# Tasks on fixed places in a software-pipelined attention kernel on one Trainium2 core

## The chip, the cores and the metric

The kernel runs on one core of one Trainium2 chip. A core has a matrix engine (TensorE, in the profile PE, with PEld for its weight loads) and three engines that work on rows of numbers: VectorE (DVE), ScalarE (ACT) and GpSimd (POOL). SyncE (SP) issues transfers. Each engine works through its own list of instructions in the order in which the program holds them, and the engines wait for each other through semaphores. Matrix products land in PSUM banks; VectorE and ScalarE carry the results from there into the on-chip memory.

The metric is the device time in microseconds, the median of several runs. A profile is taken from one execution; its "span" runs from the first to the last recorded instruction.

## The reference, cut to what matters

The input is a batch of 8 images of 32 x 32 x 256 in 32-bit floats; an image is taken as N = 1024 tokens of C = 256 channels. Layer 0 is attention with four heads, each 256 wide, layer 1 a single attention with 32-wide keys:

```python
# layer 0
qkv = einsum('bnc,cd->bnd', xf, W_qkv).reshape(B, N, 4, 3 * C)
q, k, v = split(qkv, 3, axis=-1)
atten = softmax(einsum('bihd,bjhd->bijh', q, k) * C ** -0.5, axis=2)
res = einsum('bijh,bjhd->bihd', atten, v).reshape(B, N, 4 * C)
x = einsum('bnd,dc->bnc', res, W_out) + b_out + xf
# layer 1
f, g, h = x @ Wf + bf, x @ Wg + bg, x @ Wh + bh      # 32, 32 and 256 wide
y = gamma * (softmax(g @ f.T, axis=-1) @ h) + x
```

## The kernel before, in words

**Folding.** At the start the weights of each head are multiplied together (`fold_weights`, L281): Wq with Wk, so that the scores are x (WqWk) x^T, and Wv with Wout, so that values need no projection of their own and a head's result is projected once. Four such foldings are done: head 0's ahead of the loop, the other three inside its first step.

**Seven products.** `seven` (L222) is the core of layer 0. It multiplies two matrices, each cut into 2 x 2 blocks, with seven block products in place of eight. The price is sums of blocks: four of the left matrix (`sum_a`, L192: s1, s2, s3, s4), four of the right one (`sum_b`, L202), and additions on the way out of PSUM. The seven products are made in three tasks, over three PSUM banks x, y and z:

- task one: products 1, 6 and 5 into x, y, z. Then ScalarE copies x out as e (L258), and VectorE makes u = y + e (L252). u and e are kept.
- task two: products 2 and 7, added by the matrix unit onto what stands in x and y. The first of them can only go when e has been copied. Then x goes out on ScalarE as block 11 (L264), and VectorE makes v = y + e and block 22 = z + v.
- task three: products 4 and 3, added onto y and z, which may only start once v and block 22 have read them. Then VectorE makes blocks 21 and 12.

Every sum that is made of an earlier result must therefore be ready when TensorE comes to its product: product 6 takes s2, product 5 s1, product 7 s3, product 3 s4. Where two tasks of one `seven` stand close together in TensorE's list, it waits for an evacuation; the more other tasks stand between them, the more time that evacuation has.

Three things go through `seven`: a head's queries (`queries`, L442; banks named psx_q and so on, and the four block sums `qs` as a separate list of pieces), the scores (`scores`, L472; banks psx, psy, psz), and the product of probabilities and values (`products`, L556; banks psx_y, psy_y, psz_y).

**Steps.** The work is a list of steps (L773). A unit is one head of one image (`Layer0`) or one image's layer 1 (`Layer1`), and a unit has two steps, one for each block of 512 queries. The list runs over images: heads 0 to 3 of image b, then layer 1 of image b-1. The last layer 1 follows after the loop. A step is a pipeline stage. While step i makes its own scores, it also does, for the units of steps i-1 and i-2:

- scores of step i: for each of two groups of keys three tasks of `seven`, so six (called S0a, S0b, S0c, S1a, S1b, S1c below), with exponentials on ScalarE (L489, L490, L264);
- sums of step i-1's probabilities (`sums`, L507): the four block sums as pieces of VectorE (L528), and two pieces called keys, which make the row sums of the softmax: `first` adds the s tiles (L533), `second` adds further (L538, L539), lets GpSimd add over partitions (L541), and turns the row into columns with two transfers on SP (L545, L548);
- products of step i-1 (three tasks);
- for step i-2, `invert` (L552), one reciprocal of the columns, and `project` (L577): two tasks that multiply with the folded value weights into a bank called po, each followed by two VectorE instructions (L596) that scale and add into the image's rows.

Where they fall due, a step also carries: the next head's queries and their sums; the residual in four pieces (`residual`, L378; head 0's second block); the block sums of the image as values (`value_sums`, L362); the transposes of an image (`transpose_rows`, L331, each four transposes and one ScalarE copy) and its block sums as keys (`key_sums`, L346). A layer-1 step has two score tasks of four products each with ScalarE copies (L659) and a maximum over keys (L693 to L701, with a reduction on GpSimd that shares the buffer tags `rs` and `rb` with the row sums of layer 0), five softmax pieces (subtractions on VectorE, exponentials on ScalarE), and, one step later, four products tasks of eight matmuls (`row_products`, L719); its first block also carries the values in four tasks (`values`, L628, banks named pr_v).

**What sets the order.** The order of TensorE, VectorE and ScalarE is that of the Python text: the pools are opened with a manual schedule for these three engines (L762). PSUM banks come from two pools, six for `seven` and the layer-1 scores and products, two (tag psm) for projections, transposes and values; within a pool a tile takes the next free bank. In a step, the order comes from `weave` (L746), which takes lists of tasks, each with a stretch (lo, hi) of the step. It spreads the tasks of each list evenly over the list's stretch and sorts all by that position:

```python
at = [
    (lo + (hi - lo) * (i + 0.5) / len(l), k, t)
    for k, (l, lo, hi) in enumerate(lists) for i, t in enumerate(l)
]
```

The loop over the steps (L791 to L844) fills the lists. Scores go over (0, 1), products of the step before over (0.4, 1.0), its sums over (0.08, 0.32) and (0.4, 0.7), keys over (0.7, 0.95), projections over (0.4, 0.8), queries over (0.07, 0.39). In a layer-0 step after a layer-0 step this gives S0a, S0b, S0c, S1a with the projections and products among S1a, S1b and S1c. All three products tasks of a block, and with them the two readings of its last banks, are in the one step.

Of the kernel before, what the change touches and what calls it, by code (L numbers as in the profile page):

```python
# [20 lines left out]
def kernel(  # L21
# [52 lines left out]
    B, H, W, C = x.shape  # L74
# [38 lines left out]
    rows, rows1 = {}, {}  # L113

    def load_x(b, parts=1):
        t = tile_of("rows", [P, NT, C], f"x_{b}")
        n = HT // parts
        for k in range(NBLK):
            for i in range(parts):
                nc.sync.dma_start(  # L120
                    t[:, k * HT + i * n : k * HT + (i + 1) * n, :].rearrange("p t c -> p (t c)"),
                    x_v[b][:, k, ts(i, n * C)],
                )
        rows[b] = t
# [87 lines left out]
    def a_operands(blocks, sums):  # L212
        a11, a12, a21, a22 = blocks
        s1, s2, s3, s4 = sums
        return dict(zip((1, 2, 3, 4, 5, 6, 7), (a11, a12, s4, a22, s1, s2, s3)))
# [113 lines left out]
    xT_of, x1T_of, xblocks, vblocks = {}, {}, {}, {}  # L329
# [32 lines left out]
    def value_sums(b):  # L362

        made = {}

        def piece(i):
            if i == 0:
                r = rows[b]
                t = tile_of("xt", [P, 4, NT // 2, P], f"xt_{b}")
                blocks = [r[:, ts(j, NT // 2), ts(c, P)] for j in range(2) for c in range(CC)]  # L370
                sums = [t[:, k] for k in range(4)]
                made["l"] = sum_b(sums, *blocks)
                vblocks[b] = b_operands(blocks, sums)
            made["l"][i]()

        return [partial(piece, i) for i in range(4)]

    def residual(b):  # L378


        def piece(i):
            if i == 0:
                rows1[b] = tile_of("rows", [P, NT, C], f"x1_{b}")
            nc.vector.tensor_tensor(
                rows1[b][:, ts(i, 2), :], rows[b][:, ts(i, 2), :],
                bout_sb.unsqueeze(1).broadcast_to([P, 2, C]), ALU.add,
            )

        return [partial(piece, i) for i in range(NT // 2)]
# [46 lines left out]
    class Layer0:  # L436
        def __init__(self, b, h):
            self.b, self.h, self.name = b, h, f"{b}_{h}"
            self.p, self.y, self.r = {}, {}, {}
            self.first = (b * HEADS + h) * NBLK * HT  # L440

        def queries(self):  # L442
# [64 lines left out]
        def sums(self, blk):  # L507


            n = f"{self.name}_{blk}"  # L510
            tt = nc.vector.tensor_tensor
            made = {}

            def start():
                half = NT // 2
                p = self.p[blk]
                blocks = [p[:, ts(j, half), ts(e, HB)] for e in range(2) for j in range(2)]
                t = tile_of("ss", [P, 2, half, HB], f"ss_{n}")
                s2 = tile_of("s2", [P, half, HB], f"s2_{n}")
                s3 = tile_of("s3", [P, half, HB], f"s3_{n}")  # L520
                sums = [t[:, 1], s2, s3, t[:, 0]]
                self.pblocks = a_operands(blocks, sums)
                made["t"], made["l"] = t, sum_a(sums, *blocks)

            def piece(i):
                if i == 0:
                    start()
                made["l"][i]()  # L528

            def first():  # L530
                t = made["t"]
                made["m"] = m = tile_of("m0", [P, 2, 2, HB], f"m_{n}")
                tt(m, t[:, :, 0:2, :], t[:, :, 2:4, :], ALU.add)  # L533

            def second():
                m = made["m"]
                r = tile_of("rs", [P, 2, HB], f"rs_{n}")
                tt(r, m[:, :, 0, :], m[:, :, 1, :], ALU.add)  # L538
                tt(r[:, 0, :], r[:, 0, :], r[:, 1, :], ALU.add)  # L539
                t = tile_of("rb", [P, NB], f"rb_{n}")  # L540
                nc.gpsimd.partition_all_reduce(  # L541
                    t, r.rearrange("p e i -> p (e i)"), P, bass_isa.ReduceOp.add
                )
                line = tile_of("line", [1, NB], f"line_{n}")
                nc.sync.dma_start(line, t[0:1, :])  # L545
                self.r[blk] = st = tile_of("st", [P, HT], f"st_{n}")
                with nc.allow_non_contiguous_dma(reason="a row of sums turns into columns"):
                    nc.sync.dma_start(st, line.rearrange("o (t p) -> p (o t)", p=P))  # L548

            return [partial(piece, i) for i in range(4)], [first, second]  # L550
# [5 lines left out]
        def products(self, blk):  # L556


            def out(c, e):
                if blk not in self.y:  # L560
                    self.y[blk] = tile_of("y", [P, CC, NB], f"y_{self.name}_{blk}")
                return self.y[blk][:, c, ts(e, HB)].unsqueeze(1)

            return seven(
                f"y_{self.name}_{blk}", HB, 1,
                lambda number: [
                    (0, vblocks[self.b][number][:, j, :], self.pblocks[number][:, j, :])
                    for j in range(NT // 2)
                ],
                {  # L570
                    "11": partial(out, 0, 0), "12": partial(out, 1, 0),
                    "21": partial(out, 0, 1), "22": partial(out, 1, 1),
                },
                NARROW, nc.scalar.copy,
            )
# [170 lines left out]
    def weave(*lists):  # L746
# [6 lines that stand above are left out]
        for _, _, t in sorted(at, key=lambda x: x[:2]):  # L753
            t()
# [22 lines left out]
    final = Layer1(B - 1)  # L777
# [7 lines left out]
    def is_l0(s):  # L785
        return s is not None and isinstance(s[0], Layer0)

    def step(k):
        return steps[k] if 0 <= k < len(steps) else None

    for i, (a, blk) in enumerate(steps):  # L791
        l0 = isinstance(a, Layer0)
        one, two, nxt = step(i - 1), step(i - 2), step(i + 1)
        lists = []
        if l0:
            lists.append((a.scores(blk), 0, 1))
            if a.h == 2 and blk == 0 and a.b + 1 < B:
                load_x(a.b + 1)
            if a.h == 0 and blk == 1:
                lists.append((residual(a.b), 0.3, 1))  # L800
                if a.b > 0:
                    lists.append((value_sums(a.b), 0, 0.3))
        else:
            tasks, pieces = a.scores(blk)
            lists.append((tasks, 0.02, 0.3))
            lists.append((pieces, 0.4, 1))
        if is_l0(one):
            u, k = one
            sums, keys = u.sums(k)
            lists.append((sums[:2], 0.08, 0.32))  # L810
            lists.append((sums[2:], 0.4, 0.7))
            lists.append((keys, 0.7, 0.95))
            lists.append((u.products(k), 0.4, 1.0))
        elif one is not None:
            lists.append((one[0].products(one[1]), 0.3, 1))
        if is_l0(two):
            u, k = two
            lists.append(([partial(u.invert, k)], 0.34, 0.36))
            lists.append((u.project(k), 0.4, 0.8))
        if i == 0:  # L820
            lists.append((fold_weights(1) + fold_weights(2) + fold_weights(3), 0, 1))

        if is_l0(nxt) and blk == NBLK - 1:
            queries, qsums = nxt[0].queries()
            lists.append((queries, 0.07, 0.39))
            lists.append((qsums, 0.45, 0.95))

        change = l0 and a.h == HEADS - 1
        if (change and a.b == 0 or not l0) and blk == 0 and a.b + (1 if l0 else 2) < B:
            b = a.b + (1 if l0 else 2)  # L830
            lists.append((transpose_rows(b, rows, xT_of, 0), 0.02, 0.35))
            lists.append((key_sums(b), 0.5, 0.8))

        if change and a.b > 0:
            if blk == 0:
                lists.append((transpose_rows(a.b - 1, rows1, x1T_of, 1), 0.02, 0.4))
            else:
                lists.append((nxt[0].queries(), 0.05, 0.4))
        if not l0 and blk == 0:
            lists.append((a.values(), 0.1, 0.9))  # L840
        if nxt is None:
            lists.append((transpose_rows(B - 1, rows1, x1T_of, 1), 0.82, 0.9))
            lists.append((final.queries(), 0.9, 1))
        weave(*lists)  # L844


    count = const.tile([P, 1], F32, tag="count", name="count")
# [79 lines left out]
    with tc.If(bad > 0), ExitStack() as general:  # L927
# [5 lines left out]
        for b in range(B):  # L933
# [9 lines left out]
            a = Layer1(b)  # L943
# [37 lines left out]
```

## Time and profile before

| what | value |
|---|---|
| median of 3 runs | 2511.67 us (2510.96 to 2516.9) |
| the profiled execution's own time | 2508.59 us |
| its span | 2506.8 us |
| its mean granted TensorE clock | 0.990 |
| busy: PE | 2411.3 us |
| busy: DVE | 1580.1 us |
| busy: ACT | 617.6 us |
| busy: POOL | 250.7 us |
| transfers, busiest queue | 3.1% of what 16 transfer engines could do in the span |

The page has several views. The first gives each engine's busy time, its share of the span and its number of instructions. Another follows the chain of work back from the last instruction and says how much of the span each engine held. The groups of instructions show, for a line of the kernel and an engine, what is written from what, the number of times, the busy time, the mean of one, and the idle time of that engine ahead of them with what ended most of it. A name such as psy stands for the bank y of scores, psy_y of products, psy_q of queries, po for projections, pr_v for values, pa_l for layer 1's products. The view of waits lists an engine's idle time by the instruction that ended it: total, number, longest. The view by stretch gives, for a part of the span, its length and then for PE, PEld, DVE, ACT and POOL the busy time with the number of instructions, then the granted clock, the busy share of the transfer engines and the GB/s they moved. In the timeline a line begins with its start and its duration in us; what stands in brackets is the idle time before it and what ended that.

### The profile page before, as it was taken

The page shows a single profiled execution, that of the slowest core. Times are in us where ns is not written, and L with a number is a line of the kernel's source. Part 1 is how long each engine was busy: PE and PEld are TensorE (multiplying, and loading weights), DVE is VectorE, ACT ScalarE, POOL GpSimd, SP SyncE. Part 2 cuts the span into 40 slices and gives each one's busy share as a digit, 9 for nine tenths or more (in the row PEclk, how much of TensorE's full clock was granted, in tenths as well). Part 3 has the DMA queues.
Part 4 walks back from the last instruction along what each step waited for, and adds up shares of the span by engine and source line. Part 5 has one row for each costly group of instructions (what it writes and reads, how often), then busy time and mean ns, then how long its engine had stood idle before and what let it go on. Part 6 is the DMA issues. An engine that isn't in the chain of part 4 may idle for free.

```text
span 2506.8 us, 26004 instructions
## 1 busy us (share of the span) xinstructions
PE 2411.3 (96%) x10608; PEld 1965.0 (78%) x10608; DVE 1580.1 (63%) x2477; ACT 617.6 (25%) x1001; POOL 250.7 (10%) x93
## 2 busy tenths in 40 slices
PE   8999999999999999999999999999899999999998
PEld 6788878877788777887778868788687886878876
DVE  5666666665666656666566665666666666566664
ACT  2222212232222322223222232222322223222232
POOL 0111101110111101111011110111101111011110
PEclk9999999999999999999999999999999999999999
DMA  3000000000000000000000000000000000000000
GB/s 112 1 1 1 1 17 1 1 1 29 6 1 1 1 34 1 1 1 1 34 1 1 1 1 34 1 1 1 1 34 1 1 1 1 17 1 1 1 6 30
DMA packets 43536, 23.64 MB, mean 9 GB/s; under 512 B 36048, under 2 KB 38096, under 8 KB 43408
## 3 DMA queue, kind: packets, MB, share of 16 engines
q1 hardware_dynamic: 43408, 21.90, 3.1%
q8 instruction: 85, 1.39, 0.2%
q14 instruction: 43, 0.35, 0.0%
HBM read 13.37 MB, written 8.52 MB: 9 GB/s over the span
## 4 chain that ended last, share of the span: by engine, by line
PE 80%; DVE 14%; ACT 5%; issue 1%; DMA 0%; SPq 0%; DVEq 0%; ACTq 0%
PE psy L235 12%; PE psy_y L235 11%; PE pa_l L726 9%; PE psx L235 8%; PE po L585 8%; PE psx_y L235 8%; PE psz L235 7%; PE psz_y L235 6%; PE psy_q L235 3%; PE psz_q L235 2%; PE psx_q L235 2%; DVE m L533 2%; DVE p L252 2%; ACT s_l L659 1%; DVE v L252 1%; ACT p L489 1%
## 5 line engine op out<-in xcount | busy, mean ns | idle before, releaser
L541 POOL PARTITION_ALL_REDUCE rb<-rs x64 | 214.5, 3352 | 1825.5 <-DVE rs L539 1825.5
L235 PE MATMUL psx<-q,x0T 128*128 128x256 f32 x1024 | 270.6, 387 | 24.7 <-ACT e L258 24.1
L489 ACT ACTIVATE p<-p 128x1024 f32<-128x1024 f32 x128 | 135.5, 1058 | 633.1 <-DVE p L252 633.1
L235 PE MATMUL psy<-qs,xs 128*128 128x256 f32 x1024 | 269.2, 386 | 1.7 <-DVE qs L460 1.7
L235 PE MATMUL psy_y<-s,xt 128*128 128x256 f32 x1024 | 247.4, 385 | 19.2 <-DVE s L528 19.2
L235 PE MATMUL psz<-q,xs 128*128 128x256 f32 x1024 | 262.8, 379 | 0.0
L235 PEld LDWEIGHTS psx<-q,x0T 128*128 128x128 f32 x1024 | 194.0, 192 | 72.1 <-ACT e L258 33.2
L585 PE MATMUL po<-wvo,y 128*128 128x256 f32 x1024 | 241.9, 379 | 0.0
L235 PE MATMUL psx_y<-p,x 128*128 128x256 f32 x1024 | 241.9, 379 | 0.0
L596 DVE SCALAR_TENSOR_TENSOR x<-po,inverse,x 128x256 f32<-128x256 f32 x256 | 112.0, 479 | 205.3 <-PE po L585 205.3
L235 PEld LDWEIGHTS psy_y<-s,xt 128*128 128x128 f32 x1024 | 196.8, 193 | 49.0 <-DVE s L528 18.5
L726 PE MATMUL pa_l<-v_l,s_l 128*128 128x257 f32 x1024 | 230.4, 380 | 1.8 <-DVE v_l L634 1.8
L235 PEld LDWEIGHTS psy<-qs,xs 128*128 128x128 f32 x1024 | 199.1, 195 | 30.6 <-DVE qs L460 2.1
L726 PEld LDWEIGHTS pa_l<-v_l,s_l 128*128 128x128 f32 x1024 | 194.2, 190 | 34.0 <-issue 5.2
L585 PEld LDWEIGHTS po<-wvo,y 128*128 128x128 f32 x1024 | 194.6, 190 | 26.5
L235 PEld LDWEIGHTS psx_y<-p,x 128*128 128x128 f32 x1024 | 194.6, 190 | 26.5
L235 PEld LDWEIGHTS psz<-q,xs 128*128 128x128 f32 x1024 | 194.6, 190 | 26.4
L252 DVE TENSOR_TENSOR u<-psy,e 128x512 f32<-128x512 f32 x128 | 88.5, 692 | 138.0 <-ACT e L258 78.0
L264 ACT ACTIVATE p<-psx 128x512 f32<-128x512 f32 x128 | 76.4, 597 | 321.7 <-PE psx L235 321.5
L258 ACT COPY e<-psx 128x512 f32<-128x512 f32 x128 | 74.0, 578 | 305.4 <-PE psx L235 305.4
L235 PE MATMUL psy<-qs,x0T 128*128 128x256 f32 x512 | 134.0, 384 | 13.7 <-DVE v L252 13.7
L252 DVE TENSOR_TENSOR v<-psy,e 128x512 f32<-128x512 f32 x128 | 88.5, 692 | 86.9 <-PE psy L235 86.7
(108 smaller groups left out, 3183.9 us busy)
## 6 DMA issues: line engine op xcount, KB each, us to landing
out_dram<-x SPq DMA_DIRECT2D x15, 512.0 KB, 2.6
x<-in_x_dram SPq DMA_DIRECT2D x14, 512.0 KB, 4.6
w<-in_L_conv_W_qkv_dram SPq DMA_DIRECT2D x4, 768.0 KB
x<-in_x_dram SPq DMA_DIRECT2D x4, 256.0 KB, 4.8
w<-in_L_conv_W_out_dram SPq DMA_DIRECT2D x4, 256.0 KB, 9.7
line<-rb SPq DMA_DIRECT2D x64, 2.0 KB
st<-line SPq DMA_DIRECT2D x64, 2.0 KB, 2.1
out_dram<-x SPq DMA_DIRECT2D x4, 128.0 KB, 2.3
```

The source lines that it names most:

```text
L235: nc.tensor.matmul(banks[k][:, ts(i, w)], lhsT=lhsT, rhs=rhs, start=first and n == 0, stop=True, skip_group_check=True,)
L252: nc.vector.tensor_tensor(dst, shaped(banks[k]), shaped(other), ALU.add)
L258: nc.scalar.copy(scratch("e"), banks["x"])
L264: copy(outs["11"](), shaped(banks["x"]))
L489: exp(both, both)
L533: tt(m, t[:, :, 0:2, :], t[:, :, 2:4, :], ALU.add)
L541: nc.gpsimd.partition_all_reduce(t, r.rearrange("p e i -> p (e i)"), P, bass_isa.ReduceOp.add)
L585: nc.tensor.matmul(pm[:, ts(j, C)], lhsT=self.y[blk][:, c, ts(2 * t2 + j, P)], rhs=folded[self.h][1][:, c, :], start=(c == 0), stop=(c == ...
L596: nc.vector.scalar_tensor_tensor(acc, pm[:, ts(j, C)], inverse[:, n : n + 1], acc, ALU.mult, ALU.add)
L659: nc.scalar.copy(soft.tile()[:, j0 + r, :], pm)
L726: nc.tensor.matmul(pm[:, : C + 1], lhsT=p[:, j, ts(ti, P)], rhs=v[:, j, : C + 1], start=(j == 0), stop=(j == NT - 1),)
```

## The change

The loop no longer builds lists with stretches for `weave` (which stays for what follows the loop). Each task is given a place, a number, by `put(tasks, *at)`, and the step runs its tasks sorted by place, those of equal place in the order in which they were put. In a layer-0 step the six score tasks stand at 0, 2, 4, 6, 8 and 10, the first two products tasks of the step before at 5 and 9, the projections of the step before that at 3 and 7.

Two other things change with it. The third products task of a block is no longer in the step of the other two; it comes one step later, at place 1 (0 in a layer-1 step). So `Layer0` keeps the tasks in `products_of` by block, and `pblocks`, the operands of the products, is kept by block too. And the pieces of VectorE (sums, keys, query sums, residual, value sums, key sums, `invert`, softmax pieces) each have a place of their own; s4 now goes with s1 and s2, ahead of s3, which stands at 8.2.

The whole change:

```diff
--- before.py
+++ after.py
@@ -437,6 +437,7 @@
         def __init__(self, b, h):
             self.b, self.h, self.name = b, h, f"{b}_{h}"
             self.p, self.y, self.r = {}, {}, {}
+            self.products_of, self.pblocks = {}, {}
             self.first = (b * HEADS + h) * NBLK * HT
 
         def queries(self):
@@ -519,7 +520,7 @@
                 s2 = tile_of("s2", [P, half, HB], f"s2_{n}")
                 s3 = tile_of("s3", [P, half, HB], f"s3_{n}")
                 sums = [t[:, 1], s2, s3, t[:, 0]]
-                self.pblocks = a_operands(blocks, sums)
+                self.pblocks[blk] = a_operands(blocks, sums)
                 made["t"], made["l"] = t, sum_a(sums, *blocks)
 
             def piece(i):
@@ -564,7 +565,7 @@
             return seven(
                 f"y_{self.name}_{blk}", HB, 1,
                 lambda number: [
-                    (0, vblocks[self.b][number][:, j, :], self.pblocks[number][:, j, :])
+                    (0, vblocks[self.b][number][:, j, :], self.pblocks[blk][number][:, j, :])
                     for j in range(NT // 2)
                 ],
                 {
@@ -788,60 +789,74 @@
     def step(k):
         return steps[k] if 0 <= k < len(steps) else None
 
+
+
+
     for i, (a, blk) in enumerate(steps):
         l0 = isinstance(a, Layer0)
         one, two, nxt = step(i - 1), step(i - 2), step(i + 1)
-        lists = []
+        places = []
+
+        def put(tasks, *at):
+            assert len(tasks) == len(at)
+            places.extend(zip(at, range(len(places), len(places) + len(at)), tasks))
+
         if l0:
-            lists.append((a.scores(blk), 0, 1))
-            if a.h == 2 and blk == 0 and a.b + 1 < B:
-                load_x(a.b + 1)
-            if a.h == 0 and blk == 1:
-                lists.append((residual(a.b), 0.3, 1))
-                if a.b > 0:
-                    lists.append((value_sums(a.b), 0, 0.3))
+            put(a.scores(blk), 0, 2, 4, 6, 8, 10)
         else:
             tasks, pieces = a.scores(blk)
-            lists.append((tasks, 0.02, 0.3))
-            lists.append((pieces, 0.4, 1))
+            put(tasks, *((0.5, 2.5) if blk == 0 else (0.5, 1.5)))
+            put(pieces, *((6.6, 7.6, 8.6, 9, 9.5) if blk == 0 else (5.2, 6.2, 7.8, 8.8, 9)))
+        if is_l0(two):
+            u, k = two
+            put(u.products_of[k][2:], 1 if l0 else 0)
+            put([partial(u.invert, k)], 1.1 if l0 else 0.3)
+            put(u.project(k), *((3, 7) if l0 else (2, 6) if blk == 0 else (3, 7)))
         if is_l0(one):
             u, k = one
             sums, keys = u.sums(k)
-            lists.append((sums[:2], 0.08, 0.32))
-            lists.append((sums[2:], 0.4, 0.7))
-            lists.append((keys, 0.7, 0.95))
-            lists.append((u.products(k), 0.4, 1.0))
+            u.products_of[k] = u.products(k)
+            put(sums[:2] + sums[3:], *((2.2, 3.2, 4.2) if l0 else (1.2, 2.2, 3.2)))
+            put(sums[2:3], 8.2 if l0 else 7)
+            put(keys, *((6.2, 7.2) if l0 else (5.2, 6.2)))
+            put(u.products_of[k][:2], 5, 9 if l0 else 8)
         elif one is not None:
-            lists.append((one[0].products(one[1]), 0.3, 1))
-        if is_l0(two):
-            u, k = two
-            lists.append(([partial(u.invert, k)], 0.34, 0.36))
-            lists.append((u.project(k), 0.4, 0.8))
+            put(one[0].products(one[1]), *((3, 5, 7, 9) if l0 else (1, 4, 6, 8)))
         if i == 0:
-            lists.append((fold_weights(1) + fold_weights(2) + fold_weights(3), 0, 1))
+            fold = fold_weights(1) + fold_weights(2) + fold_weights(3)
+            put(fold, *[0.3 + 0.6 * n for n in range(len(fold))])
 
         if is_l0(nxt) and blk == NBLK - 1:
             queries, qsums = nxt[0].queries()
-            lists.append((queries, 0.07, 0.39))
-            lists.append((qsums, 0.45, 0.95))
-
+            put(queries, *((1.5, 3.5, 4.5) if l0 else (2.5, 4.5, 6.5)))
+            put(qsums, *((5.2, 6.5, 7.5, 8.5) if l0 else (7.2, 7.5, 8.2, 8.5)))
+
+        if l0 and a.h == 0 and blk == 1:
+            put(residual(a.b), 5.3, 6.3, 7.3, 8.6)
+            if a.b > 0:
+                put(value_sums(a.b), 0.2, 0.4, 1.2, 1.4)
+        if l0 and a.h == 2 and blk == 0 and a.b + 1 < B:
+            load_x(a.b + 1)
         change = l0 and a.h == HEADS - 1
-        if (change and a.b == 0 or not l0) and blk == 0 and a.b + (1 if l0 else 2) < B:
-            b = a.b + (1 if l0 else 2)
-            lists.append((transpose_rows(b, rows, xT_of, 0), 0.02, 0.35))
-            lists.append((key_sums(b), 0.5, 0.8))
+        if change and a.b == 0 and blk == 0:
+            put(transpose_rows(1, rows, xT_of, 0), 2.5, 4.5, 6.5, 8.5)
+            put(key_sums(1), 8.7, 9.2, 9.5, 9.8)
+        if not l0 and blk == 0 and a.b + 2 < B:
+            put(transpose_rows(a.b + 2, rows, xT_of, 0), 1, 1.5, 3, 3.5)
+            put(key_sums(a.b + 2), 7.2, 8.2, 9.2, 9.4)
 
         if change and a.b > 0:
             if blk == 0:
-                lists.append((transpose_rows(a.b - 1, rows1, x1T_of, 1), 0.02, 0.4))
+                put(transpose_rows(a.b - 1, rows1, x1T_of, 1), 2.5, 4.5, 6.5, 8.5)
             else:
-                lists.append((nxt[0].queries(), 0.05, 0.4))
+                put(nxt[0].queries(), 1.4, 1.5, 3.5)
         if not l0 and blk == 0:
-            lists.append((a.values(), 0.1, 0.9))
+            put(a.values(), 4, 4.5, 5.5, 6.5, 8.5)
         if nxt is None:
-            lists.append((transpose_rows(B - 1, rows1, x1T_of, 1), 0.82, 0.9))
-            lists.append((final.queries(), 0.9, 1))
-        weave(*lists)
+            put(transpose_rows(B - 1, rows1, x1T_of, 1), 8.1, 8.2, 8.3, 8.4)
+            put(final.queries(), 9, 9.1, 9.3)
+        for _, _, t in sorted(places, key=lambda x: x[:2]):
+            t()
 
 
     count = const.tile([P, 1], F32, tag="count", name="count")
```

## The prediction

> **What bounds the kernel now.** First the page: busy shares, then the chain.
>
> ```profile
> PE 2411.3 (96%) x10608; PEld 1965.0 (78%) x10608; DVE 1580.1 (63%) x2477; ACT 617.6 (25%) x1001; POOL 250.7 (10%) x93
> PE 80%; DVE 14%; ACT 5%; issue 1%; DMA 0%; SPq 0%; DVEq 0%; ACTq 0%
> ```
>
> TensorE (PE) is never far from the end of anything: what can be won or lost is its idle time. Second, the waits of PE (total, times, longest, us):
>
> ```profile
> PE psx L235 <- ACT e L258: 24.1, 17, 2.5
> PE psy_y L235 <- DVE s L528: 19.2, 7, 3.0
> PE psy L235 <- DVE v L252: 13.7, 18, 0.8
> PE psy_q L235 <- DVE v_q L252: 12.4, 7, 2.7
> ```
>
> Third, busy time by step (stretch, length, busy time of PE first; the 0.95 or 1.00 is the clock): head 1's two blocks and head 2's first in batch 2, then a first layer-1 step.
>
> ```profile
> 651.80:684.70 32.90, 29.65 (x130) 25.23 (x130) 20.11 (x31) 6.04 (x10) 3.98 (x2) 0.95 0.01 1
> 684.70:718.30 33.60, 33.60 (x143) 26.97 (x142) 21.71 (x35) 7.20 (x12) 2.79 (x2) 1.00 0.01 1
> 718.30:747.80 29.50, 28.23 (x130) 24.20 (x130) 18.15 (x30) 6.04 (x10) 4.02 (x2) 1.00 0.01 1
> 842.90:874.80 31.90, 28.87 (x133) 22.94 (x133) 23.26 (x31) 10.97 (x20) 4.37 (x2) 0.95 0.01 1
> ```
>
> Second blocks have no gap; first blocks and layer 1 do. Fourth, the timeline of PE and VectorE (DVE) at one gap, which gives my prices:
>
> ```profile
> 155.78 1.03 PE L235 MATMUL psz<-q,xs 128*128 128x256 f32 x4
> 157.29 1.13 PE L235 MATMUL psx<-q,x0T 128*128 128x256 f32 x4 [0.48 <-ACT e L258]
> 158.25 1.03 PE L235 MATMUL psy<-qs,xs 128*128 128x256 f32 x4
> 160.06 1.13 PE L235 MATMUL psy<-qs,x0T 128*128 128x256 f32 x4 [0.78 <-DVE v L252]
> ```
>
> ```profile
> 159.32 0.69 DVE L252 TENSOR_TENSOR v<-psy,e 128x512 f32<-128x512 f32 x1 [0.23 <-PE psy L235]
> 160.04 0.69 DVE L252 TENSOR_TENSOR p<-psz,v 128x512 f32<-128x512 f32 x1
> 160.65 1.22 DVE L528 TENSOR_TENSOR s<-ss,p 128x1024 f32<-128x1024 f32 x1
> ```
>
> A score product takes 0.86 us from start to start (155.78 less 154.91), a products piece or projection task of eight records 1.73. The psy of 158.25 gives up its slot at 159.12; v starts 0.20 later; PE follows v's end by 0.05, and its first product then takes 0.10 longer. So this gap costs 0.20 + 0.69 + 0.05 + 0.10 = 1.05, more than the 0.78 shown idle. DVE follows a result of its own that it needs by 0.03, and overlaps an independent predecessor by 0.08. Such losses, added over all starts, are 110 us; the clock takes 22 more:
>
> ```profile
> 90.00:93.40 3.40, 0.93 (x5) 0.51 (x4) 1.88 (x4) 2.05 (x3) 0.62 (x1) 1.00 0.07 1
> 93.40:96.80 3.40, 2.82 (x7) 1.68 (x6) 1.85 (x3) 0.60 (x1) 0.00 (x0) 0.50 0.04 5
> ```
>
> In this trace every 3.4 us window with 2.2 us or more of idle slots is followed by one at clock 0.50, and none with 2.0 or less.
>
> **What the skill says.** "TensorE: Matmul & The Clock Gate", section "Architectural detail", has VectorE and ScalarE as strict first-in-first-out while TensorE only pulls weight loads ahead; the trace agrees: at 652.25 two residual adds (2.06 us) stand before a score add whose matmul was done. Its "What's actually happening" has a free-running 3.4 us window and half clock after an idle one; here 2.2 us of idleness were enough. "PSUM — Partial Sum Buffer", "Specifications", has eight banks; this kernel's pools use all (6 and 2), so a waiting bank's reader counts.
>
> **The change part by part.** The order of the built program is known; no matmul, add or transfer is added. Let S0a, S0b, S0c, S1a, S1b, S1c be the six score tasks of a layer-0 step.
>
> *Removed.* The third products task now follows S0a, so S0b no longer waits for e; and a 1.73 us or longer task stands before each S0c and S1c, so v is hidden. Per batch from 2 on that ends 3.8 us + 1.4 of clock (head 1), 1.8 (head 2), 0.55 (head 3).
>
> *Put in their place: s3.* It moves to 8.2, after S1b's v and p adds on DVE, while the second products task reads it 1.73 us after S1b. From S1b's end: 0.20 + 0.69 + 0.03 + 0.69 - 0.08 + 1.22 + 0.05 = 2.80; minus 1.73, plus 0.10: 1.18 us of PE, in every layer-0 step after a layer-0 step (57). Behind the waiting product stand S1c and the next S0a on PE, and v_y on DVE. What stands ahead of v on DVE comes on top. The rows:
>
> ```profile
> L528 DVE TENSOR_TENSOR s<-p 128x1024 f32<-128x1024 f32 x64 | 77.8, 1216 | 0.0
> L596 DVE SCALAR_TENSOR_TENSOR x<-po,inverse,x 128x256 f32<-128x256 f32 x256 | 112.0, 479 | 205.3 <-PE po L585 205.3
> L538 DVE TENSOR_TENSOR rs<-m 128x512 f32<-128x512 f32 x64 | 44.1, 688 | 3.2
> L384 DVE TENSOR_TENSOR x<-x,bout_sb 128x512 f32<-128x512 f32 x32 | 32.9, 1027 | 0.0
> L541 POOL PARTITION_ALL_REDUCE rb<-rs x64 | 214.5, 3352 | 1825.5 <-DVE rs L539 1825.5
> ```
>
> - First blocks of heads 1 and 2, from S1a's start (S1a 2.59, projection 1.73, S1b 1.73): u ends at 2.62, m 3.75, the projection's two adds (po ready 4.52) 5.39, rs 5.99, its fold 6.45. So v, which could start at 6.24, starts at 6.37: **1.31**.
> - Second blocks with queries: one more 0.69 add (qs) before v: 1.91; and the third query task, now right after S0c, comes 0.26 before v_q allows: **2.17**.
> - Head 3: first block 0.7 (a transpose task of 0.62 covers), second 1.31.
> - Head 0, second block, the dense one: from batch 2 on no projection separates S1a from S1b, and u, m, residual, qs, rs, fold, residual, qs, v, p, s3 (0.69+1.22+1.03+0.68+0.69+0.43+1.03+0.68+0.69+0.69+1.22, less overlaps = 8.46) stand against 4.12 us of PE: 4.5 lost. Four value sums ahead of v_q delay the third query task by 1.3. A gap of 4.4 leaves 2.2 or more in one of the windows it touches, so a half-clock window follows; by where it falls it costs 0.6 to 1.7, on average 1.4: **7.2** (batch 0 too; batch 1 has projections: 5.1).
> - Layer 1, first block: the first projection takes the bank of a transpose whose ScalarE copy now stands behind four score copies. These start 1.15 after their task (3.45 into the step, after the third products task), 0.48 apart, and the transpose's copy ends at 7.1, where PE is ready at 5.7: 1.5; the same for the first values task: 1.6; s3 behind the values add and a softmax piece: 1.8. **4.9** for 3.55 + 0.8 (clock).
> - Layer 1, second block: the Pool reduction shares its buffer with the softmax maximum, so it starts after the last subtraction, now 3.2 us into the step (this trace: reduction at 1183.73, column issued at 1188.16, landed 2.1 later: 6.5 in all). `invert`, put at 0.3, can run 10 us in; DVE stands still for it, and with it the maximum and the first accumulate, for whose bank the query task waits: 1.65. In layer-0 steps the column lands at S1a + 13 and `invert` comes at S1a + 18.8: nothing. The y adds late: 0.5. The next S0a waits 0.75 for qs, and S0b, with no third task between, 1.7 for e behind the last exp. **4.6** for 3.35.
>
> Sum, us: batch 0: 7.2+1.3+2.2+1.3+2.2+0.7+2.2 = 17.0 for 7.5; batch 1: 15.4 for 9.4; batches 2 to 7: 16.2 for 7.6, six times; layer 1: 9.5 for 7.7, six times; start (the folding tasks, 5.6 lost now) and tail (the last layer-1 steps have no transposes) about -4. 9.5 + 6 + 51.6 + 11 - 4 = +74. On the profiled 2508.6 (span 2506.8): 2583; the median of the runs lies 3 above: **2586**.
>
> Unseen: what a bank held by the third products task costs. Between nothing and 0.7 a step (a score add late by its length): the bank is freed by adds that end 1.5 us before need, so nothing. The ends of the clock term: 0.6 to 1.7 each.
>
> **Rivals.**
> 1. Faster (ends on the other side). DVE is 63% busy; if the pieces ahead of v run in its idle time, only the bare 1.18 remains: 64 x 1.18 = 76, plus start and tail 12, for 132: 2467. For it: second blocks have no gap now. Against: in head 0's second block 28 us of DVE work stand in 30 us. It decides if all other losses together stay under 44 us; I count 118.
> 2. Milder: `invert` and the transposes' copies are in time and no clock is lost: 6 x 1.65, 6 x 3.1 and 11 less: 2546. For it: the clock's rule is only seen up to gaps of 2.9. Against: each order stands in the program.
> 3. Banks bind, above: 57 x 0.7 more: 2626.
> 4. The order isn't what the text says: then 2512; but the built order shows the move on every engine.
>
> **Chances.** Forecast 0.75 (own range 2560 to 2610), milder 0.11, banks 0.05, faster 0.07, near no change 0.02. The range, 2548 to 2612, leaves out less than 2 in 10. What this kernel's runs can tell is about 0.3%: faster 0.07, same 0.02, slower 0.91.
>
> **What would show it.** Right: psy<-v vanishes from PE's waits and psx<-e is left at head 0's first blocks alone, some 10 us; psy_y<-s grows from 7 waits to over 60 and some 100 us; po<-x0T and pr_v<-x0T appear; head 0's second block lasts about 37 us; more 0.50 windows there. Wrong: PE waiting little on s3, or DVE running v before S1b's end. The forecast fails if adds on PSUM run shorter when they don't queue, or if the long gaps don't halve the clock.

## The result: 6.5% slower, more than twice the forecast loss

The changed kernel takes 2679.15 us (median of 4, 2678.12 to 2680.34), the kernel before 2514.28 us in the same set of runs; the ratio is 1.0654 (95% interval 1.0633 to 1.0676). Forecast were 2586 us, in a range of 2548 to 2612. The direction was right and the size wrong: +169.5 us between the two profiled executions (2678.12 and 2508.59), where the sum gave +74. That is 95 us too little.

The page of the changed kernel, busy shares and the chain:

```profile
PE 2448.9 (92%) x10608; PEld 1982.6 (74%) x10608; DVE 1649.6 (62%) x2477; ACT 621.9 (23%) x1001; POOL 252.7 (9%) x93
PE 13%; DVE 3%; ACT 0%; issue 0%; POOL 0%; ACTq 0%; DVEq 0%; POOLq 0%
```

The instruction counts are those of before. VectorE is busy 69.5 us longer for the same 2477 instructions (1649.6 less 1580.1), so some of them have become longer. The chain adds up to 16% of the span only, so its shares say little here and are not used. The waits of TensorE (total, times, longest, us):

```profile
PE psy_y L235 <- DVE s L529: 156.8, 64, 5.6
PE pa_l L727 <- POOL rb L542: 13.6, 6, 2.3
PE pr_v_l L419 <- ACT x0T L342: 9.5, 6, 1.6
PE po L586 <- ACT x0T L342: 9.5, 6, 1.6
PE psx L235 <- ACT e L258: 8.6, 6, 1.4
PE psy_q L235 <- DVE v_q L252: 8.2, 8, 1.1
```

The wait on v for the score bank psy is gone, that on e is down from 24.1 us to 8.6, and one wait has taken over: the second products task on s3, 64 times, 156.8 us. By stretch, batch 3: head 1's first block, its second block, head 2's first block, and the first layer-1 step of that batch:

```profile
1032.90:1062.80 29.90, 27.85 (x129) 24.20 (x128) 18.15 (x27) 6.04 (x10) 3.23 (x1) 1.00 0.01 1
1062.80:1101.00 38.20, 35.84 (x143) 28.00 (x142) 23.50 (x37) 7.33 (x12) 3.54 (x1) 0.96 0.01 1
1101.00:1131.00 30.00, 27.95 (x130) 24.28 (x129) 18.23 (x28) 6.04 (x10) 3.23 (x1) 1.00 0.01 1
1237.30:1269.50 32.20, 27.52 (x141) 21.88 (x140) 23.51 (x31) 10.13 (x18) 2.88 (x2) 1.00 0.00 1
```

The second block, which had no gap before (33.60 us), takes 38.20 us and stands partly at a lower clock. The timeline at one gap, head 1's first block, TensorE first, then VectorE, then GpSimd:

```profile
1055.31 1.89 PE L235 MATMUL psx_y<-p,x 128*128 128x256 f32 x8
1059.25 1.99 PE L235 MATMUL psy_y<-s,xt 128*128 128x256 f32 x8 [2.05 <-DVE s L529]
```

```profile
1055.63 0.68 DVE L252 TENSOR_TENSOR v<-psy,e 128x512 f32<-128x512 f32 x1
1056.35 0.69 DVE L252 TENSOR_TENSOR p<-psz,v 128x512 f32<-128x512 f32 x1
1056.96 2.24 DVE L529 TENSOR_TENSOR s<-p 128x1024 f32<-128x1024 f32 x1
```

```profile
1055.87 3.23 POOL L542 PARTITION_ALL_REDUCE rb<-rs  x1 [30.89 <-DVE rs L540]
```

Here is what was missed. The order is the forecast one, v, the p add, s3, and each starts where the sum put it. But s3 takes 2.24 us where 1.22 was reckoned. It runs while GpSimd adds the row sums over partitions, and that reduction had been released by the two adds just ahead of v (L539, which writes rs, and L540, which folds it in half). The groups of VectorE, by form, say that it is s3 alone of the four sums:

```profile
L529 DVE TENSOR_TENSOR s<-p 128x1024 f32<-128x1024 f32 x64 | 122.7, 1917 | 0.0
L529 DVE TENSOR_TENSOR s<-ss,p 128x1024 f32<-128x1024 f32 x64 | 77.8, 1216 | 0.2
```

Of the 64 s3, 49 start under a reduction and take 1.94 or 2.24 us; the other 15 take 1.22. The v and p adds of the same stretch, which read one operand from PSUM, keep their 0.68 and 0.69.

The Trainium skill has this on its page "SBUF — State Buffer", section "Who interferes with whom": VectorE shares one port pair with GpSimd, and "a DVE instruction with two SBUF inputs contends with a GpSimd instruction that reads SBUF". The prediction did not draw on that page. The trace agrees that one of the two is kept out and that adds with a PSUM operand are free of it. The page's section "Summary: rules for kernel authors" has the second one to issue blocked until the first finishes; there the measurement differs. The s3 above ends at 1059.20, so it ran its 1.22 us from about 1057.98, and the reduction ended at 1059.10: it was let in about 1.1 us before the reduction's recorded end.

The trace of before held the same thing. Two lines of it that the prediction did not show, VectorE and GpSimd in head 1's first block of batch 2:

```profile
652.25 2.06 DVE L384 TENSOR_TENSOR x<-x,bout_sb 128x512 f32<-128x512 f32 x1
```

```profile
651.23 3.52 POOL L541 PARTITION_ALL_REDUCE rb<-rs  x1 [30.98 <-DVE rs L539]
```

This is one residual add, as its x1 says, held by the reduction. The prediction read it as two adds in a row. It then took 1.03 us as the price of a residual add, from the group's mean; that mean is made of 24 adds of 0.68 us and 8 of 2.06, and there is no add of 1.03.

### The profile page after: what moved, and what is told of

The parts are those of the page before. It is cut to its first block, busy times and chain, and to the rows that moved or that the text cites. A ratio compares the mean times of both kernels' runs of the same rounds, so it can differ in the third digit from the quotient of the medians.

```text
span 2676.3 us, 25956 instructions
## 1 busy us (share of the span) xinstructions
PE 2448.9 (92%) x10608; PEld 1982.6 (74%) x10608; DVE 1649.6 (62%) x2477; ACT 621.9 (23%) x1001; POOL 252.7 (9%) x93
## 5 line engine op out<-in xcount | busy, mean ns | idle before, releaser
L235 PE MATMUL psy_y<-s,xt 128*128 128x256 f32 x1024 | 282.5, 425 | 156.8 <-DVE s L529 156.8
L235 PEld LDWEIGHTS psy_y<-s,xt 128*128 128x128 f32 x1024 | 208.5, 209 | 212.9 <-DVE s L529 182.5
L235 PE MATMUL psx<-q,x0T 128*128 128x256 f32 x1024 | 263.4, 380 | 8.6 <-ACT e L258 8.6
L727 PE MATMUL pa_l<-v_l,s_l 128*128 128x257 f32 x1024 | 241.8, 393 | 15.4 <-POOL rb L542 13.6
L727 PEld LDWEIGHTS pa_l<-v_l,s_l 128*128 128x128 f32 x1024 | 200.7, 197 | 55.2 <-POOL rb L542 18.4
L235 PE MATMUL psy<-qs,x0T 128*128 128x256 f32 x512 | 145.3, 411 | 0.0
L235 PEld LDWEIGHTS psy<-qs,x0T 128*128 128x128 f32 x512 | 109.9, 215 | 32.8 <-issue 9.3
```

The costliest lines, as they stand in the source:

```text
L235: nc.tensor.matmul(banks[k][:, ts(i, w)], lhsT=lhsT, rhs=rhs, start=first and n == 0, stop=True, skip_group_check=True,)
L727: nc.tensor.matmul(pm[:, : C + 1], lhsT=p[:, j, ts(ti, P)], rhs=v[:, j, : C + 1], start=(j == 0), stop=(j == NT - 1),)
```

## The experiments

Theory A: the loss is s3, late in the step and, beyond the forecast, held by the reduction. Theory B: s3 is long in its new place for another reason. Rival C: the third products task, one step later, is what costs. The figures of steps below are of batch 3. A gap is the time from the end of TensorE's last slot to its next start, plus the 0.10 us by which the first product after a gap takes longer.

**The reduction taken out, order kept.**

```diff
-                nc.gpsimd.partition_all_reduce(
-                    t, r.rearrange("p e i -> p (e i)"), P, bass_isa.ReduceOp.add
-                )
...
-                nc.sync.dma_start(line, t[0:1, :])
+                nc.sync.dma_start(line, r[0:1].rearrange("p e i -> p (e i)"))
```

The lower bound of the row sums that the kernel tests at its end (SUM_LOW) is widened with it, so that it does not turn to its general path.

> The changed kernel without GpSimd's addition over partitions of the layer-0 row sums (the transfer takes one row of the partial sums, so the rows are scaled wrongly); the order of every other instruction stays. Theory A, contention: s3 is long (1.92 us in the mean, 1.94 to 2.24 in 49 of 64) because it runs under that reduction; without it all 64 s3 take 1.22 us, PE's wait on s3 falls from 156.8 us to some 90, the half-clock windows after second blocks go, and the time is about 2570 us (2550 to 2590). Theory B, s3 is slow by itself in this place (what it reads is also read by other engines, or it follows adds on PSUM): s3 stays near 1.9 us and the time stays above 2650.

Measured: 2559.99 us, ratio to before 1.0192 (1.0173 to 1.0212). The group of s3, the wait on it, and by stretch head 1's first and second block:

```profile
L529 DVE TENSOR_TENSOR s<-p 128x1024 f32<-128x1024 f32 x64 | 77.8, 1215 | 0.0
```

```profile
PE psy_y L235 <- DVE s L529: 95.6, 64, 3.6
```

```profile
982.20:1011.10 28.90, 27.87 (x129) 24.21 (x128) 17.15 (x28) 6.04 (x10) 0.00 (x0) 1.00 0.01 1
1011.10:1046.90 35.80, 34.17 (x144) 26.81 (x143) 22.76 (x37) 7.32 (x12) 0.00 (x0) 1.00 0.01 1
```

All 64 s3 take 1.22 us. B falls. The second block shows how one cause was paid for twice. It lasts 35.80 us in place of 38.20, 2.40 less, of which the gap at s3 is 0.72 (2.62 less 1.90) and the clock 1.68: with s3 held, TensorE's idle time in one clock window passes the 2.2 us of the prediction's rule and half clock follows, with s3 not held it does not. In the changed kernel, the window with the gap and the one behind it (PE busy 1.04 of 3.40 us, then clock 0.50):

```profile
1093.10:1096.50 3.40, 1.04 (x5) 0.68 (x4) 3.18 (x4) 0.37 (x1) 2.52 (x1) 1.00 0.01 3
1096.50:1099.90 3.40, 3.40 (x9) 2.70 (x8) 0.85 (x2) 0.00 (x0) 0.00 (x0) 0.50 0.10 5
```

The two kernels' spans differ by 120.3 us (2676.3 less 2556.0). That is the price of the reduction in the changed kernel. The terms, which are estimates added up from the two traces: 61.2 of waits on s3 (156.8 less 95.6), 12.3 of waits of layer 1's first products task (13.6 less the 1.3 that are left), and 48.3 of half clock counted from start to start (59.8 less 11.5); together 121.8.

**s3 ahead of the reduction.**

```diff
-            put(keys, *((6.2, 7.2) if l0 else (5.2, 6.2)))
+            put(keys, *((6.2, 8.3) if l0 else (5.2, 7.1)))
```

> The changed kernel with the second keys piece (its two adds, the reduction and the two transfers) at 8.3 instead of 7.2, right after s3 (7.1 instead of 6.2 in layer 1). A: s3 is ahead of the reduction, takes 1.22 us, and the two adds are out of its way as well, so that each step waits 1.2 us; the time is about 2570 us (2550 to 2590). B: s3 stays near 1.9 us, the time falls only by the two adds, to some 2640.

Measured: 2540.81 us, ratio 1.0113 (1.0096 to 1.013), some 9 us under the range of A. The wait on s3, and VectorE in head 1's first block:

```profile
PE psy_y L235 <- DVE s L529: 70.3, 64, 2.5
```

```profile
998.27 0.69 DVE L252 TENSOR_TENSOR p<-psz,v 128x512 f32<-128x512 f32 x1
998.88 1.22 DVE L529 TENSOR_TENSOR s<-p 128x1024 f32<-128x1024 f32 x1
1000.01 0.68 DVE L539 TENSOR_TENSOR rs<-m 128x512 f32<-128x512 f32 x1
```

The reduction is there, behind s3, and s3 takes 1.22 us, so it is the overlap that counts. With nothing ahead of v and s3 not held, the gap is 1.18 us in all of batch 3's layer-0 steps but head 0's second block (2.80) and head 3's first (0.74). That is the bare 1.18 of the prediction.

**s3 early.**

```diff
-            put(sums[2:3], 8.2 if l0 else 7)
+            put(sums[2:3], 4.4 if l0 else 7)
```

> The changed kernel with s3 at 4.4 instead of 8.2 in layer-0 steps, behind s4 in VectorE's idle time; nothing else. If the late s3 is the cause of the loss: PE's waits on s3 are left in layer-1 steps alone (7 or 8, some 15 us), head 1's and 2's first blocks take 27.7 us instead of 29.95 and their second blocks 33.9 instead of 38.2, and the time is about 2495 us (2480 to 2515), under or at the kernel before. If s3 is only the place where another loss shows (banks held by the third products task, the pieces as such), another wait takes its place and the time stays above 2600 us.

Measured: 2482.96 us, ratio to before 0.9885 (0.9866 to 0.9904). Waits, and head 1's two blocks by stretch:

```profile
PE psy L235 <- DVE v L252: 15.5, 8, 2.1
PE pa_l L727 <- POOL rb L542: 13.6, 6, 2.3
PE psy_y L235 <- DVE s L529: 10.4, 7, 1.5
```

```profile
950.60:978.30 27.70, 27.70 (x130) 24.37 (x130) 18.43 (x31) 6.04 (x10) 3.23 (x1) 1.00 0.01 1
978.30:1012.20 33.90, 33.90 (x144) 26.90 (x143) 23.48 (x36) 7.32 (x12) 3.54 (x1) 1.00 0.01 1
```

One number moved takes back the whole loss and 29 us more (2512.18, the kernel before in this set, less 2482.96). So the place of s3 is the cause. The rest of the change shortens the first blocks as the prediction's "removed" said. The wait on v, which the changed kernel did not have, stands behind the residual pieces of head 0's second blocks.

**The third products task back in its own step.**

```diff
-            put(u.products_of[k][2:], 1 if l0 else 0)
...
-            put(u.products_of[k][:2], 5, 9 if l0 else 8)
+            put(u.products_of[k], 5, 9 if l0 else 8, 10.5)
```

> The changed kernel with the third products task back in its own step, at 10.5, behind S1c. If late s3 under the reduction is the cause: within 12 us of the changed kernel (2667 to 2691), and no wait of PE on e comes back, because the products now between S1c and the next S0a give the exponentials time. Rival C, the third task one step later is what costs (its banks, or the adds ahead of s1 on VectorE): the time falls to 2600 us or less.

Measured: 2674.53 us, ratio to before 1.0645 (1.0621 to 1.0669), 4.6 us under the changed kernel.

```profile
PE psy_y L235 <- DVE s L529: 156.8, 64, 5.6
PE psx L235 <- ACT e L258: 8.6, 6, 1.4
```

Rival C falls, and so does a reason of the prediction: the wait on e did not go because the third task follows S0a. It stays at 8.6 us with that task elsewhere. The prediction had named what fills the place between S0a and S0b; the run shows only that it is not needed there. Why 1.73 us of work after S1c serve as well (perhaps the exponentials of the last group then finish ahead of e) is not shown.

**The reduction done twice.** A second, equal call of the reduction stands behind the first.

> The changed kernel with the layer-0 reduction done twice in a row, the second with the same input and output. What it tells: how long GpSimd keeps the add out. If the add is let in when the reading part of the first reduction ends (as now, some 1.1 us before its end): s3 stays at 1.9 to 2.25 us, the second reduction starts late, and the time is within 30 us of the changed kernel's 2679. If GpSimd keeps it out until its queue is empty, s3 takes some 5 us and the time is over 2800 us. If s3's length has nothing to do with the reduction: s3 as in the changed kernel, and both reductions as long as one each.

Measured: 2700.41 us, one run. GpSimd and VectorE in one layer-0 step:

```profile
1062.78 3.23 POOL L542 PARTITION_ALL_REDUCE rb<-rs  x1 [29.28 <-DVE rs L540]
1066.10 3.23 POOL L545 PARTITION_ALL_REDUCE rb<-rs  x1
```

```profile
1063.87 2.23 DVE L529 TENSOR_TENSOR s<-p 128x1024 f32<-128x1024 f32 x1
```

s3 ends at 1066.10, at the same distance from the first reduction as with one, so it is let in before the reduction ends, whatever is queued behind. The second does not start late, against what was expected: by then s3 is done. The mean of s3 grows to 2.09 us, because in head 0's second blocks s3, free before, now starts under the second reduction and takes 2.62.

**Pieces of head 0's second block moved as well** (on top of s3 early).

```diff
+        if l0 and a.h == 0 and blk == 0 and a.b > 1:
+            put(value_sums(a.b), 4.5, 5.5, 6.5, 7.5)
...
-            put(residual(a.b), 5.3, 6.3, 7.3, 8.6)
-            if a.b > 0:
-                put(value_sums(a.b), 0.2, 0.4, 1.2, 1.4)
+            rest = residual(a.b)
+            put(rest[:2], 5.9, 9.2)
+            if a.b == 1:
+                put(value_sums(1), 1.2, 1.4, 2.4, 3.4)
+        if l0 and a.h == 1 and blk == 0:
+            put(rest[2:], 1.2, 4.5)
```

> The changed kernel with s3 at 4.4, and for head 0's second block two of the four residual pieces moved into the next step and, from the third image on, the value sums into the step before. If the pieces ahead of v and v_q are what is lost there after s3 is out of the way: PE's wait on v (15.5 us with s3 early) goes, head 0's second block takes some 28 to 29 us instead of 31.9, and the time is about 2459 us (2445 to 2472), against 2483 with s3 early alone. If they are not, it stays within 6 us of 2483.

Measured: 2462.46 us, ratio to before 0.9812 (0.9796 to 0.9828). The wait on v is gone.

**Layer-1 places too** (on top of the one before).

```diff
-            put(pieces, *((6.6, 7.6, 8.6, 9, 9.5) if blk == 0 else (5.2, 6.2, 7.8, 8.8, 9)))
+            put(pieces, *((5.1, 6.1, 7.1, 7.5, 8) if blk == 0 else (5.2, 6.1, 6.6, 7.2, 7.5)))
...
-            put(sums[:2] + sums[3:], *((2.2, 3.2, 4.2) if l0 else (1.2, 2.2, 3.2)))
-            put(sums[2:3], 4.4 if l0 else 7)
+            put(sums[:2] + sums[3:], *((2.2, 3.2, 4.6) if l0 else (1.2, 2.2, 3.2)))
+            put(sums[2:3], 5.1 if l0 else 3.4)
...
-            put(queries, *((1.5, 3.5, 4.5) if l0 else (2.5, 4.5, 6.5)))
-            put(qsums, *((5.2, 6.5, 7.5, 8.5) if l0 else (7.2, 7.5, 8.2, 8.5)))
+            put(queries, *((1.5, 3.5, 5.5) if l0 else (2.5, 3.2, 4.5)))
+            put(qsums, *((5.6, 6.5, 7.5, 8.5) if l0 else (4.6, 5.0, 5.5, 5.8)))
...
-            put(transpose_rows(a.b + 2, rows, xT_of, 0), 1, 1.5, 3, 3.5)
+            put(transpose_rows(a.b + 2, rows, xT_of, 0), 2.6, 3.5, 6.2, 6.6)
```

> As the one before, and in addition: the third query task one place later, s3 in layer-1 steps at 3.4, the transposes of layer-1 steps away from its first score task, softmax pieces and query sums earlier. What is left is some 3.4 us in each first layer-1 step. Time about 2403 us (2385 to 2420), ratio to the kernel before about 0.957. If the layer-1 edits only move the waits to other banks, it stays above 2430.

Measured: 2408.43 us, ratio to before 0.9599 (0.9583 to 0.9615), faster than both kernels. Many places were moved at once here, so the run gives no price for any one of them. Busy shares and waits:

```profile
PE 2367.1 (98%) x10608; PEld 1947.3 (81%) x10608; DVE 1609.0 (67%) x2477; ACT 620.5 (26%) x1001; POOL 251.0 (10%) x93
```

```profile
PE px L339 <- DVE x L597: 10.4, 6, 1.7
PE px L339 <- DMA x<-in_x_dram: 5.4, 3, 4.0
PE psy_q L235 <- DVE u_q L252: 4.1, 6, 0.7
```

TensorE is now busy for 98% of the span. The largest wait is a transpose in layer 1's first step, 1.7 us at a time, for a bank that a projection's adds have to read.

## Why the prediction was wrong

**The bound and the direction.** Right: TensorE's idle time is all that moved, and s3 placed after v became the one large wait.

**The bare term.** "0.20 + 0.69 + 0.03 + 0.69 - 0.08 + 1.22 + 0.05 = 2.80" is the step that failed, at its 1.22, and the like terms of the other steps (the 0.68 of qs, the 0.69 of the key sums) with it. They were taken as fixed durations. In the kernel before no s3 had run under the reduction, while the same sum put rs and the fold, whose end releases the reduction, ahead of v and so ahead of s3. In the changed kernel 49 of 64 s3 took 1.94 or 2.24 us. The table sets the forecast beside the changed kernel and the one without the reduction: us lost by TensorE per step of batch 3, half clock included:

| step | forecast | changed kernel | without the reduction |
|---|---|---|---|
| head 0, second block | 7.2 | 9.5 | 6.7 |
| head 1 and 2, first blocks, each | 1.31 | 2.32 | 1.30 |
| head 1 and 2, second blocks, each | 2.17 | 4.56 | 2.16 |
| head 3, first block | 0.7 | 1.90 | 0.88 |
| head 3, second block | 1.31 | 2.32 | 1.30 |
| layer 1, first block | 4.9 | 5.79 | 5.79 |
| layer 1, second block, and next S0a, S0b | 4.6 | 6.8 | 3.1 |
| sum | 25.7 | 40.1 | 24.7 |

Without the reduction the sum holds to 0.2 us in the plain layer-0 steps. Its total is near too, but partly by luck: layer 1's first block was put 0.9 too low, its second 1.5 and head 0's second block 0.5 too high. With the reduction, the batch loses 15.4 us more. In head 0's second block it is not s3 that is held but the query sum ahead of v, 2.73 us in place of 0.68.

**The clock.** The rule that was read off the trace of before held: in the changed kernel, the first 12 us of start-up apart, windows with up to some 2.05 us of idle time were followed by full speed and those with 2.21 or more by half. It is less sharp than it looks. Counted in the same way, three windows with 2.10 were followed by half clock in the run without the reduction, one with 2.17 by full speed with s3 early. Nor does it cover windows with layer-1 score products: in the kernel before, TensorE's record is busy for 2.74 of the 3.40 us from 878.50, and half clock follows. What such products count for is not shown. What was wrong was the input. Second blocks were put at 2.17 us of gaps, just under the bound, and came to 2.88. Half clock covers 141.4 us of the trace, 53.4 before. A range that asked which step lies close under the bound would have reached further up.

**Layer 1, second block.** The forecast loss of 1.65 behind `invert` is not in the waits of the changed kernel. The first products task lost 2.26 us earlier, and the half clock that followed cost 1.68. The view puts the wait down to the reduction, but VectorE stands between the two; its timeline:

```profile
938.59 2.73 DVE L358 TENSOR_TENSOR xs<-x0T,xs 128x512 f32<-128x512 f32 x1
941.24 0.41 DVE L252 TENSOR_TENSOR y<-psy_y,e_y 128x256 f32<-128x256 f32 x1
```

A key sum is held by the row-sum reduction (938.24 to 941.77), the y adds of the third products task stand behind it, and TensorE goes on at 941.80, 0.15 us after the first of them has read its bank. Without the reduction it starts at the same distance behind that add (1211.10 and 1211.25), and the wait falls from 13.6 us to 1.3. The forecast wait itself is not wrong, it was covered: VectorE does stand still for `invert` (3.65 us ahead of 945.63), but TensorE now comes late enough. With the keys late, where the first products task loses 0.75 us in place of 2.26, the query task waits for layer 1's first accumulate as forecast (8.3 us in all, 6 times, up to 1.8). So "banks bind" was no rival to be held against layer-0 steps, but it did happen once a batch here.

**Layer 1, first block, and the next step.** Right in kind and near in size: po and pr_v behind the transposes' copies (1.5 and 1.6 forecast, 1.86 each measured), s3 (1.8, 1.77), S0a's qs (0.75, 0.84), S0b's e (1.7, 1.69).

**What was set against it.** The forecast (2583 by the profiled execution) lies 25 us over the run without the reduction (2557.86), so two errors worked against each other: 120 us for the hold were missing and 25 us were too much, which makes the 95. For the 25 there is a likely source. The loss of before was counted from records whose slot is known, and left out what follows the layer-1 score records. The times from such a record to the next start add up to 53.6 us in the kernel before and 36.5 without the reduction: 17 us that went away and were not in the sum.

**The rivals.** "Faster" needed VectorE's pieces to cost nothing but the bare 1.18, and gave 2467. No run with s3 at 8.2 came near it. With the keys late the gap at s3 is the bare 1.18 in most layer-0 steps, and the time still is 2540.81, because the waits on po, pr_v and e stay (9.5, 9.5 and 8.6 us). With s3 and the other pieces moved 2467 was passed (2462.46). "Milder" and "no move" did not happen.

## What to carry to other kernels

Before an instruction is moved, look at what the other engines do at its new time, not only at what it waits for; a duration is a property of the place too. A group whose mean fits no single instruction (1.03 us from 0.68 and 2.06) is two groups, and the difference is a cost waiting for the next move. Where a gap comes out close under the idle time that halves TensorE's clock, price the step with full and with half clock.

## What the hardware showed that was not expected

An add on VectorE with both operands in on-chip memory that starts early in GpSimd's row-sum reduction of 128 x 512 floats (3.23 us) is let in about 1.1 us before the reduction's recorded end: 0.68 became 2.73 us, 1.22 became 1.94 to 2.62, by how early the add came. One that starts in the last 1 us is not held (layer 1's maxima in the kernel before, 1.22 us). The hold is not special to sums: in the last experiment seven s3 start under layer 1's reduction to a maximum (2.69 us) and take 2.06.

The other side pays less. In the changed kernel the 31 row-sum reductions that start while such an add runs take 3.52 to 3.61 us, the 33 that start beside an add with a PSUM operand 3.23.

Adds with an operand in PSUM are not held: v and the p adds took 0.68 and 0.69 under the row-sum reduction, the projection's scaled adds 0.47 and 0.48 under layer 1's reduction (1.78 us).
